# A four-layer graph kernel on one core: where the mask count stands on VectorE, which block goes first, and which pool holds the transposed rows

## The chip, the cores and the metric

The kernel runs on one core of one Trainium2 chip. The metric is device time in microseconds (us), and the median of three runs stands for a kernel. The profile used below is one profiled execution of the same program, with start and length of every instruction on each engine.

A core has several engines, each of which works through its own list of instructions in order: TensorE (PE; its weight loads are listed apart as PEld), VectorE (DVE), ScalarE (ACT), GpSimd (POOL) and SyncE (SP), which here only issues transfers. Transfers between the chip's main memory and the core's on-chip memory are issued by SP, ACT or POOL and carried out by 16 transfer engines.

## The reference

The input is `x`, 2708 rows of 512 numbers, and `adj`, a 2708 x 2708 matrix of zeros and ones. Four layers follow, each of the form `x = layernorm(x + layer(x, adj))`. The change is about layer 0 and the hand-over to layers 1 and 2; layers 2 and 3 are attention layers and are cut here.

```python
def _L0_gnn_ref(X, A, W_nb, b_nb, W_line, b_line, neibor_num):      # neibor_num = 64
    Ab = A > 0
    keep = Ab & (jnp.cumsum(Ab.astype(jnp.int32), axis=1) <= neibor_num)
    cnt = keep.sum(axis=1, keepdims=True).astype(X.dtype)
    nb_mean = (keep.astype(X.dtype) @ X) / jnp.maximum(cnt, 1.0)
    xj = leaky_relu(nb_mean @ W_nb.T + b_nb)
    xi = leaky_relu(X @ W_line.T + b_line)
    return xi + jnp.where(cnt > 0, xj, 0)

def _L1_gnn_ref(x, adj, W_self, b_self, W_nb, b_nb, W_comb, b_comb):
    mask = (adj > 0).astype(x.dtype)
    agg = mask @ x / jnp.maximum(jnp.sum(mask, axis=1, keepdims=True), 1.0)
    combined = jnp.concatenate([x @ W_self + b_self, agg @ W_nb + b_nb], axis=-1)
    return jax.nn.relu(combined @ W_comb + b_comb)
# ... _L2_gnn_ref and _L3_gnn_ref: attention over the same mask, with 8 heads, and a last MLP ...
x = _layernorm(x + _L0_gnn_ref(x, adj, ..., 64), axis=-1)
x = _layernorm(x + _L1_gnn_ref(x, adj, ...), axis=-1)
# ... layers 2 and 3 likewise ...
```

## The kernel before

Rows are handled in 22 tiles of 128 (the last has 20). The first stage of layer 0 goes tile by tile. It multiplies the transposed rows of x with `W_nb` and keeps the product as a sum of two parts, `yH` and `yL`; it multiplies them with `W_line`, adds the bias, applies the leaky function and x itself, and stores the result `r0`; and it loads the tile's rows of the mask, counts them on VectorE and transposes them into `maskT`, which all layers use.

```python
def keep_y(t, n, pm):
    nc.scalar.copy(yH[:n, t, :], pm[:n])
    nc.vector.tensor_sub(yL[:n, t, :], pm[:n], yH[:n, t, :].bitcast(F32))

def load_mask(t):
    m = st.tile([P, N], BF16, name="m")            # pool with two buffers
    nc.gpsimd.dma_start(m[:n], adj[t * P:t * P + n, :], ...)
    return m

def count(t, m):
    nc.vector.tensor_scalar(m[:n], m[:n], 0.0, None, op0=OP.is_gt, op1=OP.add, accum_out=cnt[:n])
    # ... four operations on cnt: iso, has, rkeep, rdeg of this tile ...

def turn(t, m):                                    # 22 transposes on TensorE, copies on ScalarE
    ...

xs = rows_of(x)
xTs = early(0, NT, lambda t: transposed(sm, ps_tr, xs(t), rows(t), "xT"))
for t in range(NT):
    n = rows(t)
    keep_y(t, n, product(xTs(t), n, wnT, 0))       # product: four fp32 matmuls of 128x512
    # ... t == 0: second weight, bias, masks 0 and 1 ...
    xT = xTs(t)
    if t + 1 < NT:
        xTs(t + 1)
    if t > 0:
        turn(t - 1, ms[t - 1])
        if t + 1 < NT:
            ms[t + 1] = load_mask(t + 1)
    pm = product(xT, n, wlT, 1)
    u = sm.tile([P, D], F32, name="u")
    nc.vector.tensor_add(u[:n], pm[:n], b_line[:n])
    leaky(u[:n], u[:n])
    nc.gpsimd.tensor_add(u[:n], u[:n], xs(t))
    nc.gpsimd.dma_start(r0_dram[t * P:t * P + n, :], u[:n])
    count(t, ms[t])
```

A scheduler orders the instructions of each engine when the program is built, so the order of this text is not the order on the engine unless something binds it.

The second stage takes blocks of four tiles (the last block has two). For each of the 22 column tiles j, TensorE makes a running count (`upper`, `below`), VectorE makes from it the kept mask `kT`, and TensorE multiplies it with yH and yL of tile j. Two generators strew other work among the steps: `finish` does bias, leaky, `r0` and layer norm of the block before, and `later` prepares weights of layer 1 (`weights1`) and vectors of the attention layers (`vectors`).

```python
cuts = [(b, min(b + 4, NT)) for b in range(0, NT, 4)]

def kept(cum, b, j):
    nc.tensor.matmul(cum[:, :w], upper, maskT[:, j, cols], ...)
    kT = st.tile([P, 512], F32R, name="kT", bufs=2)
    nc.vector.scalar_tensor_tensor(kT[:, :w], cum[:, :w], KEEP, maskT[:, j, cols], op0=OP.is_le, op1=OP.mult)
    return kT

def weights1():
    first = weight()
    for i, (w_in, b_in, wc, dst) in enumerate(...):            # two weights, 1 MB each
        load_weight(wc, l1_w_comb[i * D:(i + 1) * D, :], nc.sync)
        for m in range(KD):
            xT = transposed(sm, ps_tr, fetched(w_in, m, P), P, "xT")
            yield
            nc.scalar.copy(dst[:, m, :], product(xT, P, wc, 1))
            # ... one multiply-add of wc[:, m, :] into acc on VectorE ...
            yield

def vectors():                                                 # 24 steps
    # ... for each layer, side and k:
    nc.sync.dma_start(*w_view(wr, w_src, k))
    nc.vector.tensor_mul(wr, wr, ab)
    nc.vector.tensor_reduce(wa[:, layer, k, i, :heads], ...)
    yield

todo, later = iter(()), chain(weights1(), vectors())
for i, b in enumerate(cuts):
    for j in range(NT):
        # ... below, kept of j + 1, then for each tile of the block two matmuls (yH, yL) ...
        next(todo, None)
        if 3 <= j < NT - 2:
            next(later, None)
    # ... the block's sums leave PSUM through ScalarE; todo = finish(...)
for _ in chain(todo, later):
    pass
```

Then layer 1 projects its rows (two products per tile), multiplies with the mask, and layers 2 and 3 follow. Each layer opens its own pool `sm`; in it lies `xT`, the transposed rows of the tile at hand. The pool `ahead` stays open through all of them. In the last layer, after each block of attention, `Last.finish` takes the quotient `v`, applies elu and runs the MLP, whose output tile is `y`.

## Time and profile before

| | |
|---|---|
| time, median of three | 3542.65 us (3538.99 to 3548.86) |
| span of the profiled execution | 3543.0 us |
| TensorE busy (matmul) | 3374.2 us, 95% |
| VectorE busy | 1878.0 us, 53% |
| ScalarE busy | 1408.7 us, 40% |
| GpSimd busy | 207.0 us, 6% |
| mask loads | 21 of 677 KB and a short one, 8.1 us from issue to landing (median) |

The page cuts the span into 40 slices and gives each engine's busy share in tenths, with the clock that TensorE was granted:

```profile
PE   7778999999999999999989999999999999999998
...
DVE  4333575312323888989857988988831212212222
...
PEclk9889999999999999999989999999899999999999
DMA  4442321212212000100032000100011000000000
```

One slice is 88.6 us. The first three and a half slices are the first stage of layer 0, the next four its second stage, and layer 1 lies in slices 8 to 11. The two stretches of high VectorE load are the attention of layers 2 and 3 (eight heads each), and the last third is the last attention with the MLP. A matmul's end is modelled in the profile, so that a busy TensorE may still wait a little; gaps in its row are real.

### The profile page before, as it was taken

The numbers are of one execution on the slowest core, as the hardware profiler recorded it, in microseconds if no ns is written. First come the engines' busy times: TensorE is split into PE (matmuls) and PEld (weight loads), VectorE is DVE, ScalarE is ACT, GpSimd is POOL, SyncE is SP. The second block draws the span as 40 slices with busy tenths as digits, with TensorE's granted clock in tenths as the row PEclk, the third lists the DMA queues.
The fourth block names the chain that finished last, engine by engine and source line by source line (L and its number), as shares of the span: only waits on it lengthen the run. The fifth ranks groups of instructions, "written<-read, shape, count | busy, mean of one in ns | idle before, by whom it ended". The sixth has DMA issues, their size and how long they took to land. (4 is left out here: it accounts for less than half of the span.)

```text
span 3543.0 us, 40168 instructions
## 1 busy us (share of the span) xinstructions
PE 3374.2 (95%) x16428; PEld 1749.2 (49%) x16428; DVE 1878.0 (53%) x2353; ACT 1408.7 (40%) x1565; POOL 207.0 (6%) x320
## 2 busy tenths in 40 slices
PE   7778999999999999999989999999999999999998
PEld 4334666447865443443444443444454545454546
DVE  4333575312323888989857988988831212212222
ACT  2221000112223878878736878877740101000000
POOL 2111010101100000000011000000000000000000
PEclk9889999999999999999989999999899999999999
DMA  4442321212212000100032000100011000000000
GB/s 110 91 88 81 92 81 33 87 60 87 80 51 76 20 29 27 33 24 24 16 124 101 26 25 25 33 28 27 26 56 48 21 9 24 3 24 1 24 12 17
DMA packets 114936, 163.50 MB, mean 46 GB/s; under 512 B 39290, under 2 KB 61083, under 8 KB 114742
## 3 DMA queue, kind: packets, MB, share of 16 engines
q1 hardware_dynamic: 88454, 110.30, 9.9%
q0 software_dynamic: 14352, 42.41, 4.6%
q10 hardware_dynamic: 11936, 8.13, 0.8%
q8 instruction: 131, 2.15, 0.2%
q14 instruction: 63, 0.52, 0.0%
HBM read 130.92 MB, written 44.55 MB: 50 GB/s over the span
## 5 line engine op out<-in xcount | busy, mean ns | idle before, releaser
L551 DVE SCALAR_TENSOR_TENSOR e<-v_bc,ucol,maskT 128x1408 f32<-128x1408 f32 (+5 forms) x836 | 1193.3, 1478 | 435.8 <-PE pn L744 370.0
L559 ACT ACTIVATE c<-e,bcol 128x1300 bf16<-128x1300 f32 (+1 forms) x704 | 998.3, 1424 | 222.2 <-DVE e L551 180.8
L605 PE MATMUL po<-e,R 128*64 128x512 f32 (+4 forms) x4224 | 957.9, 566 | 3.0 <-DVE R L499 3.0
L605 PEld LDWEIGHTS po<-e,R 128*64 128x64 f32 (+1 forms) x4224 | 364.1, 140 | 498.1 <-issue 421.9
L744 PE MATMUL pn<-e,R 128*128 128x512 f32 (+3 forms) x1056 | 423.1, 542 | 1.8 <-DVE good L763 1.8
L744 PEld LDWEIGHTS pn<-e,R 128*128 128x128 f32 (+1 forms) x1056 | 190.3, 190 | 212.4 <-issue 210.3
L657 ACT ACTIVATE elu_e<-elu_e 128x512 f32<-128x512 f32 (+2 forms) x46 | 27.5, 603 | 657.5 <-DVE elu_e L656 656.0
L205 PE MATMUL pm<-w,xT 128*128 128x512 f32 (+1 forms) x384 | 203.6, 679 | 65.2 <-DVE yL L200 59.5
L491 PE MATMUL pm<-w,xT 128*128 128x512 f32 (+1 forms) x528 | 243.8, 605 | 0.0
L591 PE MATMUL pd<-c,parts_c 128*6 128x512 bf16 (+4 forms) x2112 | 222.9, 361 | 0.0
L375 PE MATMUL acc<-yH,kT 128*128 128x512 f32 x484 | 214.2, 443 | 0.0
L591 PE MATMUL pd<-maskT,parts_m 128*6 128x512 fp8e4 (+2 forms) x2112 | 210.6, 359 | 0.0
L712 PE MATMUL pl<-lin 128*128 128x256 f32 (+1 forms) x704 | 164.3, 395 | 38.2 <-DVE lin L659 38.2
L416 PE MATMUL acc<-yH,mf 128*128 128x512 f32 x484 | 192.7, 398 | 0.0
L375 PE MATMUL acc<-yL,kT 128*128 128x512 f32 x484 | 192.1, 397 | 0.0
L416 PE MATMUL acc<-yL,mf 128*128 128x512 f32 x484 | 190.2, 393 | 0.0
L712 PEld LDWEIGHTS pl<-lin 128*128 128x128 f32 x704 | 138.1, 204 | 72.3 <-DVE lin L659 49.7
L100 POOL TENSOR_TENSOR ln_rs<-ln_rs,half 128x1 f32<-128x1 f32 x88 | 52.9, 602 | 2047.1 <-DVE ln_rs L99 1367.2
L205 PEld LDWEIGHTS pm<-w,xT 128*128 128x128 f32 (+1 forms) x384 | 80.2, 215 | 179.5 <-issue 177.6
L199 ACT CAST yH<-pm 128x512 fp32r<-128x512 f32 (+1 forms) x44 | 25.7, 585 | 340.4 <-PE pm L205 340.4
L205 PE MATMUL pm<-weight,xT 128*128 128x512 f32 (+1 forms) x352 | 160.5, 598 | 0.0
L224 DVE TENSOR_SCALAR_CACHE_REDUCE m<-m 128x2708 bf16<-128x2708 bf16 (+1 forms) x22 | 65.4, 2972 | 166.2 <-DMA m<-in_adj_dram 166.2
(162 smaller groups left out, 2945.6 us busy)
## 6 DMA issues: line engine op xcount, KB each, us to landing
x<-x_dram SPq DMA_DIRECT2D x63, 256.0 KB
m<-in_adj_dram POOLq DMA_DIRECT2D x21, 677.0 KB, 8.1
v_bc<-v_dram SPq DMA_DIRECT2D x16, 704.0 KB
x_dram<-u POOLq DMA_DIRECT2D x42, 256.0 KB, 2.3
rows<-x_dram SPq DMA_DIRECT2D x42, 256.0 KB
rows<-o_dram SPq DMA_DIRECT2D x42, 256.0 KB
v_bc<-v_dram SPq DMA_DIRECT2D x16, 650.0 KB
o_dram<-o SPq DMA_DIRECT2D x32, 256.0 KB
```

Of the source, the lines that this page charges most:

```text
L100: nc.gpsimd.tensor_tensor(rs[:n], rs[:n], half[:n], OP.pow)
L205: nc.tensor.matmul(pm[:n], xT[:, k, :n], w[:, k, :], start=(k == 0), stop=(k == KD - 1))
L224: nc.vector.tensor_scalar(m[:n], m[:n], 0.0, None, op0=OP.is_gt, op1=OP.add, accum_out=cnt[:n])
L375: nc.tensor.matmul(pa[t], kT[:, (t - b[0]) * P:(t - b[0] + 1) * P], y[:, j, :], start=(j == 0 and y is yH), stop=(j == NT - 1 and y is yL))
L416: nc.tensor.matmul(pa, mf[:, j - g0, :], y[:, j, :], start=(j == 0 and y is yH), stop=(j == NT - 1 and y is yL))
L491: nc.tensor.matmul(pm[:n], xT[:, k, :n], w[:, k, :], start=(k == 0), stop=(k == KD - 1))
L551: nc.vector.scalar_tensor_tensor(e[:n, :w], v[:n, :w], ucol[:n, j, h:h + 1], maskT[:n, j, c0:c0 + w], op0=OP.max, op1=OP.mult)
L559: nc.scalar.activation(c[:n, :w], e[:n, :w], AF.Sigmoid, bias=bcol[:n, j, h:h + 1], scale=STEP)
L591: nc.tensor.matmul(pd[i][g:g + 6, :c1 - c0], lhsT, rhs, start=(j < 2 and what == 0), stop=(j >= NT - 2 and what == 1))
L605: nc.tensor.matmul(po[i][HO * k:HO * k + HO, :c1 - c0], R2[:n, j, h * HO:(h + 1) * HO], e[:n, c0:c1], start=(j == 0), stop=(j == NT - 1))
L712: nc.tensor.matmul(pl[:, :w], self.lin1[:, k, f * P:(f + 1) * P], h[:, k, :w], start=(k == 0), stop=(k == KD - 1))
L744: nc.tensor.matmul(pn[:, k, :w], lhsT, e[:n, :w], start=(j == 0), stop=(j == NT - 1))
```

## The change

The change has three parts, and one that makes room for them.

1. `count(t)` is issued behind `yL` of its own tile on VectorE. `keep_y` hands back the instruction that writes yL, and `issue_after` binds the order. It is meant to keep VectorE from standing at a mask that has not landed while other work is ready.
2. The block of two tiles goes first among the blocks of the second stage. The generators are called at other steps: nothing but the loads of the first layer-1 weight in the first block, work at every step of the second block and at every other step of the later ones. `vectors` loads one step ahead, with two buffers for the rows and two for the vector. What is left of `finish` is called from layer 1's projection and not in a row at the end; that projection moves inside the stage's scope for it.
3. `xT` is taken from the pool `ahead`, which stays, in place of each layer's `sm`. A layer's first transposes are meant not to wait for the memory of a pool that closes.
4. For the room that this takes, `v` and `y` of the last layer have one buffer each and not two.

```diff
         def keep_y(t, n, pm):
             nc.scalar.copy(yH[:n, t, :], pm[:n])
-            nc.vector.tensor_sub(yL[:n, t, :], pm[:n], yH[:n, t, :].bitcast(F32))
+            return nc.vector.tensor_sub(yL[:n, t, :], pm[:n], yH[:n, t, :].bitcast(F32))
@@ first stage
-            xTs = early(0, NT, lambda t: transposed(sm, ps_tr, xs(t), rows(t), "xT"))
+            xTs = early(0, NT, lambda t: transposed(ahead, ps_tr, xs(t), rows(t), "xT"))
@@
-                keep_y(t, n, product(xTs(t), n, wnT, 0))
+                low = keep_y(t, n, product(xTs(t), n, wnT, 0))
@@
-                count(t, ms[t])
+                with tc.issue_after(low.ins):
+                    count(t, ms[t])
@@ second stage
             cuts = [(b, min(b + 4, NT)) for b in range(0, NT, 4)]
+            cuts = cuts[-1:] + cuts[:-1]
@@ weights1
                     load_weight(wc, l1_w_comb[i * D:(i + 1) * D, :], nc.sync)
+                    if i == 0:
+                        yield
@@
-                        xT = transposed(sm, ps_tr, fetched(w_in, m, P), P, "xT")
+                        xT = transposed(ahead, ps_tr, fetched(w_in, m, P), P, "xT")
@@ vectors (cut)
-                            wr = spare[:, 1 + steps % 3, :]
+                    ab, wr = spare[:, s // KD % 2, :], spare[:, 2 + s % 2, :]
@@
+                nxt = load(0)
+                yield
+                for s, (layer, i, k) in enumerate(steps):
+                    (ab, wr), nxt = nxt, load(s + 1) if s + 1 < len(steps) else None
@@
-                    if 3 <= j < NT - 2:
+                    if i == 1 and j > 1 or i > 1 and j % 2 or i == 0 and j == 2:
                         next(later, None)
@@
-            for _ in chain(todo, later):
+            for _ in later:
                 pass
@@ layer 1's projection, now inside the stage's scope
+                nc.gpsimd.dma_start(z1_dram[t * P:t * P + n, :], u[:n])
+                next(todo, None)
@@ projection of layers 2 and 3
-            xTs = early(0, NT, lambda t: transposed(sm, ps_tr, xs(t), rows(t), "xT"))
+            xTs = early(0, NT, lambda t: transposed(ahead, ps_tr, xs(t), rows(t), "xT"))
@@ Last
-                v = sm.tile([P, 512], F32, name="v")
+                v = sm.tile([P, 512], F32, name="v", bufs=1)
@@
-                y = sm.tile([P, D], F32, name="y")
+                y = sm.tile([P, D], F32, name="y", bufs=1)
```

More of the change, by code (lines that the diff above doesn't have):

```diff
@@ L345, in vectors, with load @@
                 spare = st.tile([P, KD, D], F32, name="spare", tag="spare")
-                ab = spare[:, 0, :]
-                steps = 0
-                for layer, (w_src, w_view, a_srcs, heads) in enumerate(atts):
-                    for i in range(2):
-                        nc.sync.dma_start(ab.rearrange("p (h o) -> p h o", h=heads), a_srcs[i])
-                        for k in range(KD):
-                            wr = spare[:, 1 + steps % 3, :]
-                            steps += 1
-                            nc.sync.dma_start(*w_view(wr, w_src, k))
-                            nc.vector.tensor_mul(wr, wr, ab)
-                            nc.vector.tensor_reduce(wa[:, layer, k, i, :heads],
-                                                    wr.rearrange("p (h o) -> p h o", h=heads), AX.X, OP.add)
-                            yield
+                steps = [(layer, i, k) for layer in range(len(atts)) for i in range(2) for k in range(KD)]
+                def load(s):
+                    layer, i, k = steps[s]
+                    w_src, w_view, a_srcs, heads = atts[layer]
+                    ab, wr = spare[:, s // KD % 2, :], spare[:, 2 + s % 2, :]
+                    if k == 0:
+                        nc.sync.dma_start(ab.rearrange("p (h o) -> p h o", h=heads), a_srcs[i])
+                    nc.sync.dma_start(*w_view(wr, w_src, k))
+                    return ab, wr
+                nxt = load(0)
+                yield
+                for s, (layer, i, k) in enumerate(steps):
+                    (ab, wr), nxt = nxt, load(s + 1) if s + 1 < len(steps) else None
+                    heads = atts[layer][3]
+                    nc.vector.tensor_mul(wr, wr, ab)
+                    nc.vector.tensor_reduce(wa[:, layer, k, i, :heads],
+                                            wr.rearrange("p (h o) -> p h o", h=heads), AX.X, OP.add)
+                    yield
             todo, later = iter(()), chain(weights1(), vectors())
@@ L386 @@
                 todo = finish(ts_, us)
-            for _ in chain(todo, later):
+            for _ in later:
                 pass
-        xs = rows_of(x1_dram)
-        xTs = early(0, NT, lambda t: transposed(sm, ps_tr, xs(t), rows(t), "xT"))
-        for t in range(NT):
-            n = rows(t)
-            xT = xTs(t)
-            keep_y(t, n, product(xT, n, wnb[0], 0))
-            if t + 1 < NT:
-                xTs(t + 1)
-            pm = product(xT, n, wself, 1)
-            u = sm.tile([P, D], F32, name="u")
-            nc.vector.tensor_add(u[:n], pm[:n], bias1[:n])
-            nc.gpsimd.dma_start(z1_dram[t * P:t * P + n, :], u[:n])
+            xs = rows_of(x1_dram)
+            xTs = early(0, NT, lambda t: transposed(ahead, ps_tr, xs(t), rows(t), "xT"))
+            for t in range(NT):
+                n = rows(t)
+                xT = xTs(t)
+                keep_y(t, n, product(xT, n, wnb[0], 0))
+                if t + 1 < NT:
+                    xTs(t + 1)
+                pm = product(xT, n, wself, 1)
+                u = sm.tile([P, D], F32, name="u")
+                nc.vector.tensor_add(u[:n], pm[:n], bias1[:n])
+                nc.gpsimd.dma_start(z1_dram[t * P:t * P + n, :], u[:n])
+                next(todo, None)
         with ExitStack() as ph:
@@ L478, in project @@
             xs = early(1, NT, lambda t: source(sm, t, rows(t)))
-            xTs = early(0, NT, lambda t: transposed(sm, ps_tr, xs(t), rows(t), "xT"))
+            xTs = early(0, NT, lambda t: transposed(ahead, ps_tr, xs(t), rows(t), "xT"))
             for t in range(NT):
```

## The prediction

> **What bounds the kernel now.** I read the page first: PE is busy for 3374 of 3543 us, so time can come only from slices where its digit is under 9 or its clock under 10. The change edits layer 0, so I asked for windows of 100 us over the first 1300 us. Columns: window, length, then busy time and count of PE, PEld, DVE, ACT and POOL, then PE clock, DMA share, GB/s.

> ```profile
> 200.00:300.00 100.00, 78.94 (x316) 37.86 (x316) 35.34 (x64) 25.73 (x44) 19.13 (x24) 0.87 0.42 89
> 400.00:500.00 100.00, 93.65 (x401) 65.37 (x401) 76.96 (x140) 2.42 (x4) 9.84 (x16) 1.00 0.39 108
> 700.00:800.00 100.00, 100.00 (x273) 45.80 (x272) 18.68 (x27) 13.64 (x26) 7.56 (x14) 1.00 0.18 63
> 1000.00:1100.00 100.00, 93.14 (x398) 61.29 (x397) 26.36 (x79) 21.44 (x69) 7.40 (x20) 0.95 0.18 56
> ```

> The first stage (projections of x, counts and transposes of the mask, up to about 305 us) loses a fifth of its PE time and has a low clock. The blocks of kept neighbours (305 to 643 us) lose a little. Layer 1's projection loses nothing. Next, the waits inside the first stage (20 to 310 us; columns: total us, times, longest us), for PE and for DVE:

> ```profile
> PE pm L205 <- DVE yL L200: 59.5, 18, 5.2
> ...
> DVE m L224 <- DMA m<-in_adj_dram: 166.2, 20, 9.8
> ```

> PE waits for yL on DVE; DVE stands before the mask count (L224), waiting for a mask to land. The timeline of one tile shows why these are one chain (start, length, instruction, idle before):

> ```profile
> 144.49 0.70 POOL L218 DMA_DIRECT2D m<-in_adj_dram  x1
> ...
> 152.62 2.97 DVE L224 TENSOR_SCALAR_CACHE_REDUCE m<-m 128x2708 bf16<-128x2708 bf16 x1 [8.93 <-DMA m<-in_adj_dram]
> 155.52 0.08 DVE L224 DVE_READ_ACCUMULATOR m<-m 128x1 f32 x1
> 155.52 0.69 DVE L166 SCALAR_TENSOR_TENSOR u<-u 128x512 f32<-128x512 f32 x1
> ...
> 156.29 1.26 POOL L270 TENSOR_TENSOR u<-u,rows 128x512 f32<-128x512 f32 x1 [11.11 <-DVE u L166]
> ...
> 156.37 0.68 DVE L200 TENSOR_TENSOR yL<-pm,yH 128x512 fp32r<-128x512 f32 x1
> ...
> 157.20 5.28 PE L205 MATMUL pm<-w,xT 128*128 128x512 f32 x8 [3.19 <-DVE yL L200]
> 157.85 0.59 POOL L271 DMA_DIRECT2D r_dram<-u  x1 [0.30 <-POOL u L270]
> 158.71 0.70 POOL L218 DMA_DIRECT2D m<-in_adj_dram  x1 [0.27 <-issue]
> ```

> Follow it as a loop: a mask load is issued at 144.49, lands and lets the count start at 152.62, the count ends at 155.6, the leaky of the earlier tile stood behind it on DVE, GpSimd adds and stores the result, and only then, at 158.71, issues the next mask load. That is one trip per tile, 14.2 us, with a DMA's whole latency in it. The reason is order: in the program as built, the count of tile t+1 stands ahead of the leaky of tile t and of yL of tile t+1. So every engine runs at the pace of one transfer at a time.

> [...] the eight matmuls after 3.19 us idle take 5.28 us, after the 1.98 us at 185.78 only 3.67 us. [...] The page of this kernel has 8.1 us from issue to landing, and that is what I use. [...]

> **Part 1: the count bound behind yL of its own tile.** The built order of the changed kernel on DVE is, per tile: yL(t), count(t), add, leaky. Nothing else of this stage is new. The loop now closes over two tiles: load 8.1 + count 3.3 (with its four small ones) + add and leaky 1.3 + GpSimd 1.26 and its two issues 1.3 = 15.3 us per two tiles, 7.7 us per tile. The loop through the mask's transpose, which frees the buffer, is 0.7 + 8.1 + 3.1 + 1.5 = 13.4 us per two tiles. What does PE need? From the timeline: eight matmuls at full clock take 3.43 us from start to start, twice; the transposes of x 0.45; the 22 of the mask 1.45: together 8.8 us. So PE should set the pace again. For lateness there is room: a load is issued at the end of the transposes of tile t, and the next use of its buffer begins two tiles less 1.45 us later, at 16.1 us; minus issue 0.7 and count 3.2, a landing of up to 12 us would still be in time. The transfer engines: in this stage the DMA share is 0.42 of 14.2 us, so 6.0 us of all sixteen per tile, and 6.0 of 8.8 is 68%.

> The sum: the line product of the first tile starts at 26.8 us now; without two counts in front of a weight copy on DVE I put it at 22. Then 21 periods of 8.8 and a last 4.3 (product and short transpose): 22 + 185 + 4 = 211 us. I allow 4 us for imperfect periods and take 215, where the kernel before reaches 305: **minus 90 us**.

> **Part 2: the two-tile block first, loads a step ahead.** Now PE stands at the start of the blocks, because the first kT waits on DVE behind a multiply that waits for a 1 MB weight:

> ```profile
> 314.36 0.49 DVE L333 TENSOR_SCALAR u<-w,bc 128x512 f32<-128x512 f32 x1 [8.01 <-DMA w<-in_L_gnn_W_comb_dram]
> ...
> 315.36 0.67 DVE L289 SCALAR_TENSOR_TENSOR kT<-pm,maskT 128x512 fp32r<-128x512 f32 x1
> ```

> PE loses about 9.5 us there. In the changed order that multiply still stands ahead of the first kT, but its load is issued behind the last yH product, some 6 us before PE gets to the blocks, and ahead of other loads in its queue: I leave 5 us of loss (the second 1 MB load included), a gain of 4 to 5. The vectors stage (400 to 480 us) loses 6.35 us of PE time by its windows, where kT waits behind multiplies that wait for small loads; fewer per block and a step ahead, I leave 3: gain 3. The two-tile block now has no finish of four tiles to do; free of that its step takes 1.16 us, which is just PE's need (4 x 0.233 + 2 x 0.11), and it loses about 5 us now between 608 and 627. But seven multiplies of 0.74 us each now stand between its kT's: gain 3. The drain at 641 us, now strewn over layer 1's projection, where DVE is 19% busy: gain 2. Together **minus 13 us**, of the 26 us by which the 338 us of this stage exceed my count of its matmuls (312).

> **Part 3: transposed rows in a pool that stays.** At each layer's start the pool of xT is new and waits for what lay in its memory. For layer 2 this is on PE's path:

> ```profile
> 1037.71 1.89 PE L485 MATMUL psd<-wa,xT 128*128 128x16 f32 x8 [6.86 <-ACT xT L109]
> ```

> and the cold clock after it adds 3.5 us (1.89 instead of 0.96, then 6.19 instead of 3.60). With xT in a pool that stays, about 1 us of copy remains: **minus 9 us**. At layers 3 and 4 the waits (11.08 and 2.75 us) are for the rows themselves; no gain. The price is one buffer fewer for v and y at the end. v: DVE goes multiply, min, max, next multiply, last step; every exponential still lies behind a multiply, and the final step comes about 0.6 us later per block, while PE gets earlier lines to work on: 0, give or take 3. y: the next one comes seven us later, a store of 2 to 3 us is done: 0. The order of all other attention work is the same in both kernels.

> Sum: 3542.65 - 90 - 13 - 9 = 3430.65; I say **3432 us**.

> **Rivals.** *The loads become the bound.* If masks on one queue, with stores and rows between, take 10 to 11 us per tile, PE waits before the mask's transposes and the first stage ends near 250 us: gain 55 there, total about 3467. For it: while a mask moves, the sixteen engines are 70 to 100% busy in windows of 1 us. Against it: 6.0 us of work in a period of 8.8, and two buffers that now really overlap.
> *The wait moves to the add's side.* The add and leaky of tile t now stand behind count(t); with a late mask they delay GpSimd's add, the store and the next load, and the loop of one trip per tile comes back, as 13 to 14 us. Then only parts 2 and 3 are left, about 3515. Against it: in the new order the load belongs to a tile two trips away, and count(t+1) no longer stands ahead of leaky(t). I give it 5%.
> *DVE becomes the bound in the blocks.* In the third block 15 multiply-and-reduce pairs (1.3 us each) and the finish of four tiles (about 14 us) join 22 kT's (0.6 us each): 47 of the block's 51 us. With bubbles it may exceed that, and part 2 would be 0 or even plus 5: about 3445.

> **Range and chances.** Part 1 alone has most of the uncertainty: minus 55 to minus 95. Parts 2 and 3: minus 10 to minus 27. The low end, 3410, takes all of them at their best but a little; the high end, 3466, is the first rival. 2% is 3471.8 us, which only the second rival or a mix reaches: faster by over 2% 0.92, within 0.07, slower 0.01.

> **What would show it.** Right: mask loads 8.5 to 9.5 us apart; PE's wait for yL gone; PE clock 0.97 or more up to the end of the first stage; the first kT near 215 us; DVE's wait for masks far below 166 us; the first matmul of layer 2's vectors within 2 us of the transposes before it. Wrong: mask landings of over 12 us with PE waiting in front of L238 (first rival), or periods still near 14 us (second). A clock that stays near 0.87 without gaps would also break part 1, by up to 30 us.

## The result, and the profile after

The changed kernel takes 3412.27 us (median of 4 runs, 3405.34 to 3412.58); the kernel before takes 3541.41 us beside it (4 runs, 3538.99 to 3548.86). The ratio is 0.963, with a 95% interval from 0.961 to 0.965: 129 us less. Predicted were 3432 us with a range from 3410 to 3466; the median lies at the range's low end, and the ratio times 3541.41 us, 3409 us, is just below it. The direction and the mechanisms of the three parts were right; the sum was some 18 us too small (111 us of gain for 129).

First the same kind of window as before, 100 us of the first stage (window, length, busy time and count of PE, PEld, DVE, ACT and POOL, PE clock, DMA share, GB/s):

```profile
100.00:200.00 100.00, 100.00 (x470) 53.69 (x469) 60.52 (x105) 41.20 (x69) 28.53 (x34) 1.00 0.64 135
```

In the first stage PE now works through 470 records in 100 us where it had 316, at full clock, and it has become the bound. The waits inside that stage (20 to 218 us) show where the old wait went:

```profile
PE pm L205 <- ACT xT L109: 0.7, 1, 0.7
...
DVE yL L200 <- ACT yH L199: 53.1, 21, 2.7
```

PE's 59.5 us for yL are gone, and DVE's 166 us for masks with them. DVE now waits for ScalarE's yH instead, 2.5 us per tile, which costs nothing, because PE is busy meanwhile. The timeline of one tile, to be held against that of before:

```profile
142.47 0.69 DVE L200 TENSOR_TENSOR yL<-pm,yH 128x512 fp32r<-128x512 f32 x1 [2.58 <-ACT yH L199]
...
143.08 2.96 DVE L224 TENSOR_SCALAR_CACHE_REDUCE m<-m 128x2708 bf16<-128x2708 bf16 x1
...
143.88 0.70 POOL L218 DMA_DIRECT2D m<-in_adj_dram  x1 [1.76 <-PE acc L238]
...
148.03 0.69 DVE L166 SCALAR_TENSOR_TENSOR u<-u 128x512 f32<-128x512 f32 x1
...
152.71 0.70 POOL L218 DMA_DIRECT2D m<-in_adj_dram  x1 [1.76 <-PE acc L238]
```

The count (L224) follows yL directly and finds its mask in place. Mask loads are issued 8.83 us apart, which is PE's own need, and what they wait for is PE's transposes of the mask before (L238). The page gives 6.2 us from a mask's issue to its landing, where before had 8.1.

At the start of the blocks and of layer 2, the two places where the prediction saw PE stand:

```profile
219.59 0.27 PE L379 MATMUL pm<-maskT,below 128*128 128x256 fp8e4 x1 [1.22 <-DVE kT L291]
...
221.68 0.27 PE L379 MATMUL pm<-maskT,below 128*128 128x256 fp8e4 x1 [0.59 <-DVE kT L291]
...
924.20 1.06 PE L497 MATMUL psd<-wa,xT 128*128 128x16 f32 x8 [0.24 <-ACT xT L109]
```

The first two waits are what is left of the 9.5 us that the prediction counted there; the third stood at 6.86.

To see where the 132 us between the two profiled executions come from, I cut each span at the first PE instruction of every stage. In brackets stands the time in that stage during which the trace records the granted clock as half.

| stage | before | after | difference | predicted |
|---|---|---|---|---|
| first stage | 305.8 (65) | 218.1 (10) | -87.7 | -90 |
| blocks | 337.3 (14) | 318.6 (0) | -18.8 | -13 |
| layer 1: projection | 160.7 (0) | 160.3 (0) | -0.4 | 0 |
| layer 1: mask product, and layer 2: projection | 343.9 (10) | 333.9 (0) | -10.0 | -9 |
| layer 2: attention | 661.9 (96) | 655.8 (81) | -6.1 | 0 |
| layer 3: attention | 645.1 (74) | 636.5 (55) | -8.6 | 0 |
| projections of layers 3 and 4 | 219.6 (11) | 219.6 (11) | 0.0 | 0 |
| last attention and MLP | 868.6 (82) | 868.0 (82) | -0.6 | 0 |

Two rows are off: the blocks by 6 us, and the attention of layers 2 and 3 by 15. The change touches no instruction of the attention but the buffer in which xT of its projection lies. The rows of the two attention layers, as windows:

Kernel before:

```profile
1147.76:1809.65 661.89, 649.19 (x4501) 269.90 (x4501) 567.08 (x429) 518.47 (x399) 2.94 (x5) 0.93 0.09 28
1917.16:2562.25 645.09, 641.42 (x4488) 265.15 (x4489) 564.87 (x425) 519.32 (x401) 0.00 (x0) 0.94 0.08 26
```

Changed kernel:

```profile
1030.89:1686.65 655.76, 642.73 (x4501) 266.50 (x4501) 566.95 (x429) 518.29 (x399) 2.93 (x5) 0.94 0.09 28
1794.68:2431.15 636.47, 632.99 (x4489) 261.74 (x4489) 564.67 (x425) 519.26 (x401) 0.00 (x0) 0.96 0.08 26
```

DVE and ACT do the same work in the same busy time, to 0.2 us. Only PE's busy time and its clock differ. So the question for the experiments: do these 15 us belong to the change, and to which part?

### The profile page after: what moved, and what is told of

Same layout as the page of the kernel before. It is cut to its first block, busy times and chain, and to the rows that moved or that the text cites. A ratio compares the mean times of both kernels' runs of the same rounds, so it can differ in the third digit from the quotient of the medians.

```text
span 3410.7 us, 40155 instructions
## 1 busy us (share of the span) xinstructions
PE 3322.6 (97%) x16428; PEld 1731.3 (51%) x16428; DVE 1883.0 (55%) x2353; ACT 1408.6 (41%) x1565; POOL 209.9 (6%) x320
## 5 line engine op out<-in xcount | busy, mean ns | idle before, releaser
L503 PE MATMUL pm<-w,xT 128*128 128x512 f32 (+1 forms) x528 | 241.3, 600 | 0.0
L205 PE MATMUL pm<-w,xT 128*128 128x512 f32 (+1 forms) x384 | 175.3, 599 | 1.4 <-ACT xT L109 1.4
L205 PE MATMUL pm<-weight,xT 128*128 128x512 f32 (+1 forms) x352 | 160.5, 599 | 0.0
L734 PE MATMUL pl<-lin,gT 128*128 128x512 f32 (+1 forms) x352 | 153.0, 592 | 0.0
L291 DVE SCALAR_TENSOR_TENSOR kT<-pm,maskT 128x512 fp32r<-128x512 f32 (+1 forms) x132 | 84.7, 641 | 122.7 <-PE pm L289 122.4
L737 DVE TENSOR_TENSOR y<-pl,x 128x512 f32<-128x512 f32 (+1 forms) x22 | 15.2, 691 | 243.9 <-PE pl L734 239.9
```

The lines of the kernel that those rows point to most:

```text
L205: nc.tensor.matmul(pm[:n], xT[:, k, :n], w[:, k, :], start=(k == 0), stop=(k == KD - 1))
L503: nc.tensor.matmul(pm[:n], xT[:, k, :n], w[:, k, :], start=(k == 0), stop=(k == KD - 1))
L734: nc.tensor.matmul(pl[:n], gT[:, f, (t - t0) * P:(t - t0) * P + n], self.lin2[:, f, :], start=(f == 0), stop=(f == KF - 1))
```

## The experiments

Two theories of the attention were held against each other. A: the granted clock there depends on when its instructions fall, so the 15 us belong to no part. B: part 3 gives the buffers of the attention other places, and that makes it faster. For the rest stands the additive theory: each part is worth what its own stage shows.

### One part at a time

`e1_count_only` is before with these lines, `e2_count_undone` is after with the last two of them taken back:

```diff
-                keep_y(t, n, product(xTs(t), n, wnT, 0))
+                low = keep_y(t, n, product(xTs(t), n, wnT, 0))
@@
-                count(t, ms[t])
+                with tc.issue_after(low.ins):
+                    count(t, ms[t])
```

`e3_pool_only` is before with `transposed(ahead, ...)` for `transposed(sm, ...)` in the first stage, weights1 and the projections, and `bufs=1` for v and y. `e4_blocks_only` is after with parts 1 and 3 undone.

e1, expected:

> The kernel before plus part 1 alone (count bound behind yL of its own tile). Every theory has the first stage end near 218 us (before 305.8) and the kernel near 3453 us. Theory A, the clock: the attention of layers 2 and 3 (before 658.4 and 645.1 us, changed 652.3 and 636.5) belongs to no part of the change; it depends on where in time the work falls, so here, 88 us earlier with untouched pools, either length may come up and each stays between 634 and 660. Theory B, the pools: the shorter attention comes from the other places that part 3 gives the buffers; then both lengths are those of before, 658 and 645 within 2 us, and the kernel lies at 3453 to 3456.

e2, expected:

> The changed kernel without part 1: the order of the counts is again left to the scheduler, parts 2 and 3 stay. If the parts add up, the first stage ends at 304 to 306 us and the kernel at 3412 + 88 = 3500 us, within 8. If a piece of the gain in the blocks needs part 1 (loads of the blocks that run early only when the first stage is short), the second stage is longer than the 318.6 us of the changed kernel by 3 or more. Theory A (clock): attention spans anywhere between 634 and 660. Theory B (pools): 652 and 636 within 2, as in the changed kernel.

e3, expected:

> The kernel before plus part 3 alone (xT from the pool that stays, one buffer for v and for y). Layer 2's first vector product no longer waits 6.9 us for xT; layer 1's mask product also starts earlier: together 10 us by the trace of the changed kernel. Theory A (clock): 3541 - 10 = 3531 us, give or take 8 for the attention. Theory B (pools): 3541 - 10 - 15 = 3516 us, with attention spans of 652 and 636 us.

e4, expected:

> Part 2 alone (two-tile block first, loads a step ahead, the rest of finish strewn over layer 1's projection); counts and pools as in the kernel before. The second stage takes 319 to 321 us in place of 337.3, the first stays at 305, layer 2's start keeps its wait of 7 us: 3541 - 18 = 3523 us. Theory A: give or take 8 for the attention. Theory B: attention spans of 658 and 645 within 2, so 3521 to 3526.

Measured (ratio to before with its 95% interval; stages from one profile each):

| kernel | median, us | ratio | first stage | blocks | layer 1 product, layer 2 projection | attention 2 | attention 3 |
|---|---|---|---|---|---|---|---|
| before (25 runs) | 3539.6 | 1 | 305.8 | 337.3 | 343.9 | 661.9 | 645.1 |
| e1, part 1 | 3442.2 | 0.972 (0.970 to 0.975) | 219.2 | 330.6 | 343.6 | 649.3 | 649.6 |
| e4, part 2 | 3523.3 | 0.995 (0.994 to 0.997) | 307.2 | 324.4 | 343.5 | 661.6 | 645.1 |
| e3, part 3 | 3516.7 | 0.995 (0.993 to 0.997) | 310.7 | 339.1 | 333.9 | 645.0 | 638.9 |
| e2, parts 2 and 3 | 3506.7 | 0.991 (0.988 to 0.994) | 312.7 | 320.9 | 333.9 | 649.3 | 636.5 |

Each part does in its own stage what it should: the first stage is part 1, the 10 us at layers 1 and 2 are part 3, and part 2 alone brings the blocks down by 13, as the prediction had it (e4's expectation of 319 to 321 us, taken from the changed kernel, was missed by 3). Without part 1 the first stage takes anything from 305.8 to 312.7 us, so e2's 304 to 306 was missed too. e1 came out 11 us under the 3453 expected: 6.7 in the blocks, where nothing was expected of it, and the rest mostly in the attention. B falls with e1: its pools are those of before, and it has 649.3 and 649.6 us where before has 661.9 and 645.1. (The expectations give layer 2's attention as 658.4 before and 652.3 changed; that is the same stretch, cut 3.5 us earlier at its end.) For e3 the median alone, 3516.7, would have spoken for B. But the clock moves it: its 16 runs reach from 3504.6 to 3536.8 us, and its mean granted clock goes from 0.960 down to 0.951 with them (correlation -0.98). One program, unchanged, scatters by 32 us with the clock.

The blocks hold a surprise: part 1 alone takes 6.7 us from them. The reason is a chain across the border of the two stages. Kernel before:

```profile
300.99 2.96 DVE L224 TENSOR_SCALAR_CACHE_REDUCE m<-m 20x2708 bf16<-20x2708 bf16 x1 [4.84 <-DMA m<-in_adj_dram]
...
303.88 0.68 DVE L166 SCALAR_TENSOR_TENSOR u<-u 128x512 f32<-128x512 f32 x1
...
304.65 1.26 POOL L270 TENSOR_TENSOR u<-u,rows 128x512 f32<-128x512 f32 x1 [7.08 <-DVE u L166]
...
305.93 0.33 SPq L144 DMA_DIRECT2D rows<-in_L_gnn_W_self_dram  x1
...
306.35 0.39 SPq L140 DMA_DIRECT2D w<-in_L_gnn_W_comb_dram  x1
```

Part 1 alone:

```profile
210.96 0.69 DVE L166 SCALAR_TENSOR_TENSOR u<-u 128x512 f32<-128x512 f32 x1
...
213.71 0.38 SPq L140 DMA_DIRECT2D w<-in_L_gnn_W_comb_dram  x1
...
219.90 0.49 DVE L334 TENSOR_SCALAR u<-w,bc 128x512 f32<-128x512 f32 x1 [0.57 <-DMA w<-in_L_gnn_W_comb_dram]
```

Before, the last count waits for its mask, the leaky stands behind it, GpSimd's add (L270) behind that, and only that add frees the rows buffer for which SyncE's queue is held up; the 1 MB weight is the next load in the queue and goes out at 306.35, when PE is already at the blocks. With part 1 it goes out at 213.71, 5.5 us ahead of PE, and the 8.01 us that DVE waited for it become 0.57. So part 1 alone takes most of the loss at this border.

Part 2 alone does what the prediction said of it: the load goes out at 301.10, 6.1 us ahead of the blocks, and 5 us of loss are left:

```profile
307.51 0.61 POOL L271 DMA_DIRECT2D r_dram<-u  x1 [0.30 <-POOL u L270]
...
311.56 0.48 DVE L336 TENSOR_SCALAR u<-w,bc 128x512 f32<-128x512 f32 x1 [3.91 <-issue]
...
313.02 0.37 PE L378 MATMUL pm<-maskT,below 128*128 128x256 fp8e4 x1 [5.55 <-DVE kT L290]
```

What is left is not the second 1 MB load, though, as the prediction had it. The view names no releaser for the multiply (L336), but by the semaphore in the trace it waits for the store of r0, which goes out at 307.51 and lands at 311.48, and that store stands behind the same late count. How late it is differs between profiles: with parts 2 and 3 (e2) PE's wait is 1.66 us, and with all three 1.22. So at this border parts 1 and 2 overlap: part 1 alone makes the blocks 6.7 us shorter, but only 2.3 (320.9 to 318.6) where parts 2 and 3 are there already.

### Where the clock falls

If the clock is at fault, something other than idle time must bring it down in the attention, for PE shows hardly a gap there: in layer 3 of the kernel before it is busy for 641.4 of 645.1 us. Here are 8 us windows over the end of the same pair of heads in layer 3, kernel before:

```profile
2068.00:2076.00 8.00, 8.00 (x38) 4.67 (x32) 3.59 (x3) 6.34 (x8) 0.00 (x0) 0.53 0.01 2
2076.00:2084.00 8.00, 8.00 (x23) 3.76 (x25) 2.55 (x4) 0.65 (x1) 0.00 (x0) 0.50 0.00 0
```

and the changed kernel:

```profile
1950.00:1958.00 8.00, 8.00 (x60) 3.78 (x56) 4.87 (x3) 8.00 (x10) 0.00 (x0) 1.00 0.19 77
1958.00:1966.00 8.00, 8.00 (x55) 3.17 (x54) 6.72 (x9) 4.33 (x4) 0.00 (x0) 1.00 0.01 2
```

PE is busy throughout in both. Before it does 61 matmul records in 16 us at half clock, after it does 115 at full clock.

| start after a grid line, us | half clock at this place |
|---|---|
| 3.03, 3.39, 0.02, 0.19, 0.26, 0.29, 0.34, 0.39, 0.42 | yes, all nine (13.7 or 17.1 us) |
| 0.73, 0.74, 0.76, 0.81, 0.81, 1.42, 1.46 | no, all seven |

One cut on the circle of 3.413 us parts all sixteen. The cut belongs to this place: at the fourth pair of each layer no stretch comes in any of the sixteen, and they start between 2.97 and 0.35. What lies in the step of the grid before such a stretch? The last row tile: the graph's last 20 rows. Groups of matmuls by shape in the kernel before (line, engine, operation, shapes, count, busy us, mean ns, idle us):

```profile
L605 PE MATMUL po<-e,R 128*64 128x512 f32 x2688 | 757.8, 625 | 3.0 <-DVE R L499 3.0
...
L605 PE MATMUL po<-e,R 20*64 20x512 f32 x128 | 33.5, 600 | 0.0
```

The 20-row matmuls take as long as the others and use 20 of the array's 128 rows. At the end of each pair of heads there are twelve such records in a row, and six more for the divisors. At the pair shown above, the 20-row records hold PE for 0.69 of the step from 2065.08 us in the kernel before, and half clock follows for 17.07 us from 2068.49. In the changed kernel they fall into two steps, from 1946.56 us on, and hold 0.58 and 0.49 of them; the clock stays at 1.00.

### Filling up the last row tile

```diff
+    nc.gpsimd.memset(R2[:, NT - 1, :], 0.0)
+    nc.gpsimd.memset(bcol[:, NT - 1, :], 0.0)
@@ weights, above, the divisors, the heads' loop and last_attention (in short)
-            n = rows(j)
+            n = P
```

The mask's 108 spare rows were zero already, so these rows add nothing to any sum.

Filled-up kernel before, expected:

> The kernel before, with the last row tile of the attention layers filled up: its 20 rows of weights, scores and values become 128 rows, of which 108 hold zeros, so that TensorE multiplies with all its rows there; results are unchanged and no instruction is added but two small memsets. Theory A1: the half-clock stretches in the attention start where a window of 3.41 us is mostly filled by the 20-row matmuls (whether it is depends on where the window's grid falls); then without such matmuls half of the half-clock time of layers 2, 3 and of the last attention (96, 74 and 82 us) goes, at 0.44 us saved per us: 55 us, 3541 to about 3485. Theory A2: they come from the four-column matmuls at a head pair's end; then nothing changes, 3541 within 10. Theory B (places of buffers): also nothing, and attention spans of 658 and 645 stay.

Filled-up changed kernel, expected:

> The changed kernel with the same filling up. A1: about 45 us less than 3412, so 3367; and the attention of layers 2 and 3 is equal to that of the filled-up kernel before within 4 us each, so that the difference between the two kernels is 88 (first stage) + 19 (blocks) + 10 (starts of layers) = 117 us and the other 15 are gone. A2 and B: 3412 within 8, and the difference of 15 us in the attention stays.

Measured: 3467.1 us for the filled-up kernel before (ratio 0.981, 0.978 to 0.984) and 3346.3 us for the filled-up changed one (0.946, 0.943 to 0.949), which is 74 and 66 us less than without. Windows of the attention of layers 2 and 3, filled-up kernel before:

```profile
1147.31:1770.06 622.75, 609.69 (x4501) 256.45 (x4501) 566.96 (x429) 517.18 (x399) 2.94 (x5) 0.98 0.10 30
1878.32:2488.55 610.23, 606.50 (x4488) 253.54 (x4489) 564.77 (x425) 518.22 (x401) 0.00 (x0) 0.99 0.09 28
```

filled-up changed kernel:

```profile
1027.31:1648.54 621.23, 607.50 (x4501) 255.78 (x4501) 566.75 (x429) 517.17 (x399) 2.93 (x5) 0.98 0.10 30
1757.17:2367.25 610.08, 606.42 (x4488) 253.32 (x4489) 564.78 (x425) 518.26 (x401) 0.00 (x0) 0.99 0.08 28
```

Two things follow. The 20-row matmuls bring the clock down: with the same number of instructions on every engine, the half-clock time of the two layers falls from 170 to 41 us, and their length by 74 (A1; A2, by which nothing would change, is refuted for the long stretches). Luck with the grid does not explain it: in none of the six filled-up profiles (four more follow below) does a stretch of 13.7 or 17.1 us come at the second pair, though one of them starts at 0.26 us, inside the upper row of the table. And with the clock's dips gone the attention is the same in both kernels within 1.6 us, where it differed by 15. The two kernels are now 120.8 us apart, where 117 were expected. The gain was larger than the 55 and 45 us expected. Of 39 us saved in layer 2, the expected 0.44 us per us of half clock (layer 3 of the two unfilled kernels has 8.6 us for 19.4 us of it) explains 31; about 8 us per layer are something else that these matmuls cost.

What stands in the step before a drop can be counted in the traces of before and after, in these two layers. A record holds PE here from its start to the start of the next. Of the 670 steps at full clock, 29 are followed by half clock. Where the 20-row matmuls hold two thirds of the step or more, half clock followed in 16 of 17 cases (0.68 to 0.82 of the step in those 16). Of the other 653 steps it followed 13, and each of these 13 holds four-column closing matmuls (L623/L635). So do the steps before all 36 drops that are left in the six filled-up profiles, and A2 may hold for these; no run took the closing matmuls away. Nor did a run try numbers of rows between 20 and 128, so the counts are of these matmuls and say nothing of others.

### The parts again, with the clock quiet

In filled-up kernels the runs of one program lie within 9 us, so the parts can be weighed by the stopwatch. These three are e1, e3 and e4 with the same filling up.

Part 1, expected:

> The filled-up kernel before (3467.1 us) plus part 1 alone. Additive theory: first stage 211 to 219 us in place of 306.0 (its start hangs on when the second weight lands), second stage 330 in place of 336.8 as in the unfilled run with part 1 alone, nothing later: 3467 - 91 - 7 = 3369 us, within 4. Rival: part of the 120.8 us between the two filled-up kernels comes only with all parts together; then this run is above 3375 and the three parts alone add up to less than 112.

Part 3, expected:

> The filled-up kernel before plus part 3 alone. Layer 1's mask product 227.2 in place of 233.9 and layer 2's projection 106.7 in place of 109.9, as in the unfilled run: 10 us. The unfilled run showed the first stage 5 us longer; if that was a late weight by chance, here 3457 us; if the pool does it, 3462.

Part 2, expected:

> The filled-up kernel before plus part 2 alone. Second stage 324 in place of 336.8 us (with 5.5 us of TensorE's wait left at its start, as in the unfilled run), nothing else: 3467 - 13 = 3454 us, within 4.

| filled-up kernel | median, us | range | against filled-up before |
|---|---|---|---|
| before | 3467.1 | 3465.8 to 3474.6 | |
| part 1 alone | 3369.0 | 3367.0 to 3370.2 | -98.1 |
| part 2 alone | 3455.4 | 3454.2 to 3457.7 | -11.8 |
| part 3 alone | 3456.7 | 3455.5 to 3459.6 | -10.4 |
| all three | 3346.3 | 3341.9 to 3348.5 | -120.8 |

The three parts alone add up to 120.3, so within the runs' scatter nothing is shared and nothing needs the others. Stage by stage a little is: from the blocks' start to the end of layer 1's projection the profiles give minus 5.8, minus 13.8 and plus 0.7 us for the parts alone, and minus 17.1 for all three, 2 less than their sum. All three expectations were met within 2 us. Part 1's 98 are 91 in the first stage (306.0 to 214.6) and 6 in the blocks (336.8 to 331.0).

### The order of the blocks, the second weight, and the best version

`e5_order_undone` is after without `cuts = cuts[-1:] + cuts[:-1]`. `w1_masks_later` is after with a binding for the first two mask loads; `best` is that with the last tile filled up:

```diff
             def load_mask(t, behind=None):
                 m = st.tile([P, N], BF16, name="m")
+                if behind is not None:
+                    nc.gpsimd.tensor_copy(m[:1, :1], behind[:1, :1])
@@ t == 0; landed is the last piece of the second weight
-                        ms[i] = load_mask(i)
+                        ms[i] = load_mask(i, landed)
```

e5, expected:

> The changed kernel with the two-tile block last again; the generators' calls keep the step numbers of the change. The prediction gave the order of blocks 3 us of its own (no finish of four tiles beside the short steps) and the calm boundary 4 to 5, because only loads are asked for in the first block. If so: the second stage 322 to 327 us in place of 318.6, the kernel 3416 to 3421, plus or minus 6 for the clock in the attention. Rival: the order is worth nothing by itself, the second stage stays within 2 us of 318.6.

w1, expected:

> The changed kernel, with the first two mask loads held back until the rows of the second weight have landed (one copied number binds them). If the two masks in front of that weight on the transfer engines are why TensorE waits 5.8 and 1.4 us for it at 17 and 19 us, the first product starts 3 to 5 us earlier than 20.3 us and the first stage ends at 213 to 215 us in place of 218.1. Rival: the weight waits for its own buffers and its own 1 MB, and the masks come later for nothing: first stage 218 to 222 us.

best, expected:

> The changed kernel with the last row tile filled up and the first two masks held back until the second weight has landed. Against the filled-up changed kernel (3346.3; first stage 212.9 in its profile, a lucky start) the first stage takes 210 to 212 us in every run: 3340 to 3346 us, that is 0.944 to 0.946 of the kernel before and about 2% under the changed kernel.

e5: the blocks take 322.8 us in place of 318.6, within what was expected of the order, and layer 1's projection 158.6 in place of 160.3, so 2.5 us remain. By the stopwatch this is lost in the clock: 3403.6 us (ratio 0.963, 0.960 to 0.966; runs from 3392 to 3413). Inconclusive as a time.

w1: the first stage takes 211.1 us, 7 less than the changed kernel's profile, 2 us better than the 213 to 215 expected. The time, 3396.3 us (0.961, 0.956 to 0.966; runs from 3382 to 3412), is unclear for the same reason. `best` takes 3338.0 us (0.943, 0.939 to 0.947), a little under what was expected, with a first stage of 209.8 us; the filled-up changed kernel has 3346.3 and 212.9, so in these two profiles the binding is worth 3 of the 8 us between them, and 4 lie in the attention, where the clock differs again. This is the fastest version here, about 74 us under the changed kernel. What the binding changes is seen at the second weight. Changed kernel:

```profile
16.96 1.09 PE L119 MATMUL ps_tr<-ident,wr 128*128 128x128 f32 x4 [5.78 <-DMA wr<-in_L_gnn_W_line_dram]
```

best:

```profile
12.33 0.63 PE L119 MATMUL ps_tr<-ident,wr 128*128 128x128 f32 x4 [1.03 <-DMA wr<-in_L_gnn_W_line_dram]
```

## Where the prediction was right, and which of its steps failed

**The mechanism of part 1 was right.** The one trip per tile is gone; the period is 8.83 us against 8.8 worked out; PE sets the pace; the DMA share is 0.64 against 0.68; no engine waits for a mask. From the start of the first line product to the end of the stage, all seven profiles with part 1 take 188.4 us, against 189 worked out, so the 4 us added for imperfect periods were not needed. Against them stood the start, which the prediction had wrong: 22 us, from 26.8 (27.2 in the trace) less the two counts in front of a weight copy. The counts are gone from there, and the start is still at 24.6 to 30.8 in the five profiles without a binding, because PE then waits for the second weight itself, which lands behind the first two masks. With these held back, the start is at 22.7 and 21.4.

**The size of part 1 was wrong: "minus 90", measured minus 98.** This is the first mis-sized term. It left out what the late count does beyond its stage: the 6 us at the border of the blocks, through leaky, add and rows buffer to the weight's load, or through the store of r0. The prediction saw the wait there, booked 4 to 5 us of it under part 2 and left 5 standing; in the changed kernel 1.8 are left, and the blocks fall by 18.8 in place of 13. In the first stage the filled-up pair has minus 91 and the first pair of profiles minus 87.7; its length without part 1 lies between 305.8 and 312.9 in seven profiles, so no more than this can be read from one pair.

**Part 2, "minus 13": minus 11.8, right.** The 5 us left at the border by part 2 alone are 5.55 in the first trace and 3.10 in the filled-up one. **Part 3, "minus 9": minus 10.4, right**, 6.7 of it in layer 1's mask product with the start of layer 2, and 3.2 in layer 2's projection. One buffer for v and y costs nothing that the last stage shows (868.6 and 868.0 us).

**"The order of all other attention work is the same in both kernels": the order is, the time was not.** This is the second mis-sized term: 0 in the sum, minus 15 between the two profiles and about minus 8 between the medians (129 without and 121 with the last tile filled up). It is an effect of where the work falls on the clock's grid, and no merit of a part: with the last tile filled up the two layers are within 1.6 us. The prediction looked for a low clock behind idle gaps alone; in these layers it falls while PE is busy (8.00 of 8.00 us at 0.50). The range from 3410 to 3466 held no allowance for that, though 16 runs of one program (e3) differ by 32 us in step with the clock.

So of 129 us the sum explained 112 (90, 13 and 9); 8 more were part 1's, and about 8 the clock's. **The rivals** did not come up: no landing of a mask held PE up, the add side did not close a loop, and in the fullest stretch of the blocks (345 to 396 us) DVE is busy 43.5 us of 51 while PE idles 0.7.

What stays open: whether a program's place on the grid is chance or partly fixed. The 25 runs of before beside e1 to e4 lie between 3526 and 3550, the four of the changed kernel within 7 us, and those of e3 in two groups around 3510 and 3533. The 51 us of half clock that are left in the last stage were not looked into either.

## What to carry to other kernels

A wait for a load at the head of an engine's queue can be worth more than the time shown at it (here 6 us more, in the next stage): follow what stands behind it, engine by engine, until it reaches the next stage's loads, and book the gain where the wait began. Before small gains are weighed on a kernel that TensorE bounds, look at the granted clock and at the runs' scatter, and take the disturbance away in both kernels (here by filling up a ragged tile with zeros); then parts of 10 us can be measured in four runs. Read PE's clock even where PE shows no gap: here it was busy for 8.00 of 8.00 us with 23 matmul records at a clock of 0.50, and with 55 at 1.00.

## What the runs showed of the hardware

- PE dropped to half clock while busy: 8.00 of 8.00 us at 0.50 in the attention of the kernel before. At the second pair of heads, 13.7 to 17.1 us at half clock came, or nothing, with starts 0.31 us apart on a grid of 3.413 us (0.42 and 0.73). In the traces of before and after, steps that 20-row matmuls held for two thirds or more were followed by half clock in 16 of 17 cases. Filling these rows up with zeros took 129 of 170 us of half clock away in two layers, for two memsets.
- Runs of one program differed by 32 us of 3510 in step with the mean granted clock (0.951 to 0.960).
- VectorE and ScalarE did not pay for the 108 added rows: in layer 2's attention VectorE is busy for 567.08 us without and 566.96 with them, ScalarE for 518.47 and 517.18.
